# Eight steps of a spiking recurrence take their last rows from SyncE's single-row copies, and the first tables are loaded ahead of those copies

## The chip, the cores and the metric

The kernel runs on one core of one Trainium2 chip. The metric is the time of one execution on the device in microseconds (us), the median over several runs. A profile is one execution taken by the hardware profiler; its span is the time from the first to the last instruction.

In this document PE is TensorE (matrix products and transposes), DVE is VectorE, ACT is ScalarE, POOL is GpSimd and SP is SyncE. SP computes nothing here: it issues DMA transfers, loads registers and waits.

## The reference

`seq` has 1024 rows of 50 item numbers, `emb_table` has 100001 rows of 128 float32 values, `lengths` has 1024 numbers.

```python
emb = emb_table.at[0].set(0.0)
e = emb[seq]                                   # 1024 x 50 x 128: a gather
prefix = jnp.cumsum(e, axis=1)
uF = prefix / minimum(1..T, lengths)           # T = 50
y = batch_norm(uF, over the batch) * gamma + beta
def step(v, x):                                # 50 steps, one after another
    v = v + (x - v) / 2.0
    spike = (v >= 1.0)
    return v - spike * 1.0, spike
uF_out = spikes.mean(axis=0)                   # 1024 x 128
scores = uF_out @ emb.T                        # 1024 x 100001: 409.6 MB
```

## The kernel before, in words

The work has two stages. In the first, 50 steps run in order. In the second, the counts of spikes are multiplied with the whole table, and 409.6 MB of scores are stored.

**A step of the recurrence.** The 1024 sequences stand as eight blocks of 128. `gather(t)` fetches the table rows of step t: for each block GpSimd issues one indirect DMA (line 250) into a tile `e`, 128 rows of 512 bytes. There are two tiles `e` in turn, so the gathers of step t + 2 wait until TensorE has read those of step t. At line 395 TensorE transposes the eight blocks and adds them to the running sums in `pre` (two halves of 512 columns); at line 351 it adds a correction for table row 0. VectorE scales the sums (`uF`, line 409) and takes statistics (412, 424), ScalarE takes the root and the normalized input (428, 435, 458), VectorE updates the potential `v` (367, 370, 461).

**The rows of SyncE.** In the steps listed in `BY_SYNC`, GpSimd gathers seven blocks only. The 128 rows of the eighth block are fetched by SyncE, one DMA for each row (`fetch_singles`, lines 263 to 274). For each 32 rows (`AT_ONCE`) a register load (line 268) brings 32 byte offsets; then each row has a register move and a DMA of 512 bytes (line 271). The rows land in one of four slots of the tile `held_rows`, set i in slot i % 4, and in the step's line 395 TensorE transposes that slot in place of the eighth block. The first set is written into SyncE's queue before step 0; set i + 1 is written into it after step `BY_SYNC[i]`. That is the order within the queue; a later set does not wait for that step on the chip unless its slot is still to be read.

**The table parts.** The table is cut into 98 parts of 1024 rows. The first 40 are loaded by SyncE (line 150), in six groups of six parts, 3072 KB each, and four more parts, and are held on chip until used. `EARLY` tells how many of the six groups are written into SyncE's queue ahead of the first set of single rows. The others follow the last set. At step 44 a further load is written into the queue (line 488) over parts that have been used by then.

**The second stage.** For each part `prepare` transposes it and splits it in two (lines 179, 195, 196). For each part and each of the eight blocks of sequences TensorE makes products (line 203), VectorE and ScalarE scale them in turn into a tile `o` (lines 626, 628), and SyncE stores the tile (line 212). A tile `o` is free again when its store has landed. Later parts are loaded from ScalarE's queue, in places GpSimd picks rows (line 125, with small copies at line 117 between them).

Queues: SyncE's queue takes its DMAs in the order in which the program writes them. The program is scheduled by hand; no planner reorders it.

Of the kernel before, what the change touches and what calls it, by code (L numbers as in the profile page):

```python
# [34 lines left out]
SPLITS = (0, 2, 0, 1, 0, 1, 0, 0)  # L35
PIECES = {(3, 7): 1, (4, 0): 1, (7, 7): 1, (8, 0): 3, (8, 1): 3, (8, 2): 3}

BY_SYNC = (12, 22, 31, 40, 48)
AT_ONCE = 32
EARLY = 2  # L40

SPARED = 120
PICKED = range(42, 97, 3)
# [7 lines left out]
def rec_kernel(  # L51
# [55 lines left out]
    def group(g):  # L107
        at = g if g < AHEAD else AHEAD - 2 + g % 2
        r = rowp.tile([P, GROUP, HALF], F32, tag=f"rows{at}", name=f"rows_{g}")
        for k in range(GROUP):  # L110
            rows[g * GROUP + SHIFT + k if g else k + ASIDE * (k >= TWICE)] = r[:, k, :]
        return r
# [30 lines left out]
    def fetch(r, k, q, n):  # L143

        engine = nc.sync if q < held else nc.scalar
        n = min(n, parts - q)
        whole = n - (size(q + n - 1) < HALF)
        wide = whole - (whole == n and q + whole - 1 in PICKED)
        if wide:
            engine.dma_start(  # L150
                out=r[:, k : k + wide, :],
                in_=table[q * HALF : (q + wide) * HALF, :].rearrange("(q p k) d -> p q (k d)", p=P, k=KQ),
            )
        if wide < whole:
            pick(r[:, k + wide, :], q + wide, engine)
        if whole < n:
            full, rest = divmod(size(parts - 1), KQ)
            c1 = (parts - 1) * HALF
            r = r[:, k + whole, :]
            if rest:  # L160
                at = full - full % 32
                nc.vector.memset(r[at : at + 32, :], 0.0)
                engine.dma_start(
                    out=r[full : full + 1, : rest * D],
                    in_=table[c1 + full * KQ : N, :].rearrange("(o k) d -> o (k d)", o=1),
                )
            if full:
                engine.dma_start(
                    out=r[:full, :],
                    in_=table[c1 : c1 + full * KQ, :].rearrange("(p k) d -> p (k d)", k=KQ),  # L170
                )
# [43 lines left out]
    with ExitStack() as ph:  # L215
# [23 lines left out]
        fetch(first, TWICE, SHIFT, GROUP - TWICE)  # L239
        for g in range(1, EARLY):  # L240
            fetch(group(g), 0, g * GROUP + SHIFT, GROUP)
# [5 lines left out]
        def gather(t):  # L247
            es[t] = gp.tile([P, B], F32, tag="e", name=f"e_{t}")
            for n in range(NB - (t in BY_SYNC)):
                nc.gpsimd.indirect_dma_start(  # L250
                    out=es[t][:, n * P : (n + 1) * P],
                    out_offset=None,
                    in_=table,
                    in_offset=bass.IndirectOffsetOnAxis(ap=idx[:, n, t : t + 1].bitcast(U32), axis=0),
                )
# [7 lines left out]
        def fetch_singles(i):  # L263
            t = BY_SYNC[i]
            rows_of = held_rows[:, i % (BANK // P) * P :][:, :P]
            singles[t] = rows_of
            for p0 in range(0, P, AT_ONCE):
                nc.sync.load(regs, starts[t : t + 1, p0 : p0 + AT_ONCE])  # L268
                for k, reg in enumerate(regs):
                    at = nc.sync.snap(reg, donate=True, min_val=0, max_val=(N - 1) * row_bytes)  # L270
                    nc.sync.dma_start(  # L271
                        out=rows_of[p0 + k : p0 + k + 1, :].bitcast(U8),
                        in_=byte_rows[bass.ds(at, row_bytes)].rearrange("(o b) -> o b", o=1),
                    )
# [112 lines left out]
        for t in range(T):  # L387
# [26 lines left out]
            if t + 2 < T:  # L414
                gather(t + 2)
            if t in BY_SYNC[:-1]:
                fetch_singles(BY_SYNC.index(t) + 1)
                if t == BY_SYNC[-2]:
                    for g in range(EARLY, AHEAD):
                        fetch(group(g), 0, g * GROUP + SHIFT, GROUP)  # L420
# [252 lines left out]
```

## Time and profile before

| | |
|---|---|
| runs | 1722.19, 1728.29 and 1725.5 us, median 1725.5 us |
| the profiled execution | 1711.72 us, span 1710.0 us |
| mean granted clock of TensorE | 0.777 |
| busy: PE, PEld, DVE, ACT, POOL | 1078.7, 816.4, 947.2, 675.8, 432.7 us |
| DMA | 488.23 MB, 286 GB/s on the mean |

How to read it. The page cuts the span into 40 equal slices; a digit is the busy share of an engine in that slice, in tenths. A group line gives the source line, the engine, the operation, output<-input, the count, then busy time and mean ns of one; behind it the idle time before these instructions, and what ended it. A line of the waits gives who waited for whom: total us, times (and the longest). A line of the time order gives start and duration in us, and in square brackets the idle time ahead of it with what ended it; consecutive instructions of one line are merged into one row with a count, which for a queue such as SPq tells from when to when it issued. The instructions of one source line are listed with their shortest, median and longest duration in ns, and the first and last start. A table of windows gives for each stretch its length, each engine's busy time (with the number of instructions), the granted clock, the DMA engines' busy share and the GB/s.

### The profile page before, as it was taken

How to read it: one execution, taken by the hardware profiler on the slowest of the kernel's cores; microseconds unless marked ns; L12 is line 12 of the kernel's file. 1: busy time of each engine (PE TensorE's matmuls, PEld its weight loads, DVE VectorE, ACT ScalarE, POOL GpSimd, SP SyncE). 2: the span in 40 equal slices, each digit the busy share in tenths (PEclk: the TensorE clock that was granted, in tenths of full speed). 3: DMA queues.
4: the chain of work that ended last, by engine and by line, in shares of the span. 5: the costliest groups of instructions: out<-in, count | busy, mean ns of one | idle time of the engine just before them, and what ended most of it. 6: DMA issues, size and time to landing. Idle time of an engine off the chain costs nothing.

```text
span 1710.0 us, 13726 instructions
## 1 busy us (share of the span) xinstructions
PE 1078.7 (63%) x4465; PEld 816.4 (48%) x4465; DVE 947.2 (55%) x1129; ACT 675.8 (40%) x701; POOL 432.7 (25%) x462
## 2 busy tenths in 40 slices
PE   3332331331312416898998888788888888888984
PEld 2111210211211215676777676676666666666763
DVE  4565752773744824556755555555555555555653
ACT  2232321331322413454554444444454444444442
POOL 7666664664664610000000100100100100100000
PEclk7555555555555557999999999898998998999998
DMA  6111111111111129999999999999999999999998
GB/s 223 44 48 47 45 46 34 42 47 32 49 45 34 49 108 409 413 402 423 422 404 430 424 424 426 429 428 423 428 427 426 422 429 424 427 425 430 424 429 379
DMA packets 55612, 488.23 MB, mean 286 GB/s; under 512 B 12527, under 2 KB 13424, under 8 KB 34420
## 3 DMA queue, kind: packets, MB, share of 16 engines
q1 hardware_dynamic: 33472, 431.19, 59.9%
q0 software_dynamic: 16656, 35.60, 7.1%
q10 hardware_dynamic: 5412, 20.56, 2.9%
q8 instruction: 35, 0.57, 0.1%
q14 instruction: 37, 0.30, 0.1%
HBM read 77.69 MB, written 409.60 MB: 285 GB/s over the span
## 4 chain that ended last, share of the span: by engine, by line
DMA 34%; PE 18%; DVE 4%; ACT 3%; issue 3%; SPq 3%; ACTq 0%; DVEq 0%
DMA scores<-o 34%; PE po L203 17%; SPq L271 3%; DVE o L626 3%; ACT o L628 2%; PE pt L179 1%; DVE pairs L196 1%; DMA scores<-two_rows 1%; ACT pairs L195 0%; ACT hi L195 0%; DVE lo L196 0%; SPq L268 0%; PE warm L380 0%; ACT third L195 0%; DVE uF L409 0%
## 5 line engine op out<-in xcount | busy, mean ns | idle before, releaser
L626 DVE TENSOR_SCALAR o<-po 128x1024 f32<-128x1024 f32 x378 | 452.6, 1214 | 322.7 <-DMA scores<-o 158.2
L628 ACT ACTIVATE o<-po 128x1024 f32<-128x1024 f32 x379 | 380.6, 1025 | 494.0 <-DMA scores<-o 324.3
L250 POOL DMA_INDIRECT e<-in_L_rec_emb_table,idx x395 | 375.9, 952 | 228.4 <-issue 110.4
L203 PE MATMUL po<-pairs,countB 128*128 128x512 f32 (+1 forms) x1120 | 290.6, 406 | 42.0 <-ACT o L628 40.3
L203 PE MATMUL po<-pairs,countC 128*128 128x512 f32 (+1 forms) x840 | 242.9, 437 | 60.9 <-ACT o L628 53.7
L203 PEld LDWEIGHTS po<-pairs,countB 128*128 128x128 f32 x1120 | 209.1, 191 | 104.5 <-ACT o L628 55.0
L351 PE MATMUL pre<-zT,ls 128*128 128x512 f32 x100 | 78.6, 788 | 276.7 <-DVE uF L409 176.9
L203 PEld LDWEIGHTS po<-pairs,countC 128*128 128x128 f32 x840 | 169.3, 209 | 114.6 <-ACT o L628 65.1
L409 DVE SCALAR_TENSOR_TENSOR uF<-rlen,pre 128x512 f32<-128x512 f32 (+1 forms) x101 | 68.1, 674 | 235.7 <-PE pre L395 119.2
L125 POOL DMA_INDIRECT rows<-in_L_rec_emb_table,picks x19 | 18.6, 981 | 691.6 <-PE pt L179 688.8
L351 PEld LDWEIGHTS pre<-zT,ls 128*128 128x128 f32 x100 | 29.1, 293 | 317.8 <-DVE uF L409 202.0
L428 ACT ACTIVATE r<-mv,eps 128x1 f32<-128x1 f32 x50 | 14.7, 295 | 346.2 <-DVE mv L424 183.6
L196 DVE TENSOR_TENSOR pairs<-pt,pairs 128x1024 fp32r<-128x1024 f32 x70 | 85.2, 1218 | 96.0 <-ACT pairs L195 95.9
L395 PE MATMUL pre<-ident,e 128*128 128x128 f32 x395 | 102.7, 423 | 25.3 <-DMA e<-in_L_rec_emb_table,idx 13.5
L179 PE MATMUL pt<-ident,rows 128*128 128x128 f32 (+1 forms) x768 | 105.4, 283 | 8.8 <-issue 4.9
L179 PEld LDWEIGHTS pt<-ident,rows 128*128 128x128 f32 (+1 forms) x768 | 95.1, 148 | 25.3 <-issue 11.0
L395 PEld LDWEIGHTS pre<-ident,e 128*128 128x128 f32 x395 | 82.0, 218 | 44.8 <-DMA e<-in_L_rec_emb_table,idx 21.1
L395 PE MATMUL pre<-ident,held_rows 128*128 128x128 f32 x5 | 2.4, 476 | 140.2 <-DMA held_rows<-in_L_rec_emb_table 140.2
L203 PE MATMUL po<-hi,countB 128*128 128x512 f32 x208 | 85.8, 413 | 7.8 <-ACT o L628 7.7
L203 PE MATMUL po<-hi,countC 128*128 128x512 f32 x156 | 69.2, 444 | 27.9 <-ACT o L628 27.0
L195 ACT CAST pairs<-pt 128x1024 fp32r<-128x1024 f32 x70 | 70.0, 1012 | 41.8 <-PE pt L179 41.0
L203 PE MATMUL po<-lo,countB 128*128 128x512 f32 x208 | 83.9, 403 | 0.0
(103 smaller groups left out, 1080.7 us busy)
## 6 DMA issues: line engine op xcount, KB each, us to landing
scores<-o SPq DMA_DIRECT2D x93, 3072.0 KB
scores<-o SPq DMA_DIRECT2D x29, 1536.0 KB
scores<-o SPq DMA_DIRECT2D x28, 1024.0 KB
scores<-o SPq DMA_DIRECT2D x8, 2896.5 KB
rows<-in_L_rec_emb_table ACTq DMA_DIRECT2D x19, 1024.0 KB
rows<-in_L_rec_emb_table SPq DMA_DIRECT2D x5, 3072.0 KB
held_rows<-in_L_rec_emb_table SPq DMA_DIRECT2D x640, 0.5 KB
e<-in_L_rec_emb_table,idx POOLq DMA_INDIRECT x395
```

Source lines behind the costliest of these rows:

```text
L125: nc.gpsimd.indirect_dma_start(out=r, out_offset=None, in_=runs, in_offset=bass.IndirectOffsetOnAxis(ap=which[: r.shape[0], j : j + 1].bit ...
L179: nc.tensor.transpose(pt[:, k0 : k0 + pw], r[:pw, k0 : k0 + D], ident[:pw, :pw])
L195: nc.scalar.copy(vh, vp)
L196: nc.vector.tensor_tensor(vl, vp, vh.bitcast(F32), ALU.subtract)
L203: nc.tensor.matmul(po[:, :kw], lhsT=counts[n], rhs=part[:, k0 : k0 + kw], start=j == 0, stop=j == 1,)
L250: nc.gpsimd.indirect_dma_start(out=es[t][:, n * P : (n + 1) * P], out_offset=None, in_=table, in_offset=bass.IndirectOffsetOnAxis(ap=idx[: ...
L271: nc.sync.dma_start(out=rows_of[p0 + k : p0 + k + 1, :].bitcast(U8), in_=byte_rows[bass.ds(at, row_bytes)].rearrange("(o b) -> o b", o=1),)
L351: nc.tensor.matmul(pre[h], lhsT=l, rhs=zT[:, h * BANK : (h + 1) * BANK], start=t == 0, stop=False, skip_group_check=True,)
L395: nc.tensor.matmul(pre[h][:, k : k + P], lhsT=singles[t] if h * BANK + k + P == B and t in singles else e[:, h * BANK + k : h * BANK + k + P],
L409: nc.vector.scalar_tensor_tensor(uF[:, some], rlen[:, some], 1.0 / (t + 1), pre[h][:, ready], ALU.max, ALU.mult)
L626: nc.vector.tensor_scalar_mul(o[:, h0 : h0 + hw], po[:, :hw], 1.0 / T)
L628: nc.scalar.mul(o[:, h0 : h0 + hw], po[:, :hw], 1.0 / T)
```

## The change

Three more steps take their eighth block from SyncE: eight sets instead of five, used in steps 11 to 48. All six groups of held table parts are written into SyncE's queue ahead of the first set.

```diff
-BY_SYNC = (12, 22, 31, 40, 48)
+BY_SYNC = (11, 17, 22, 28, 33, 38, 43, 48)
 AT_ONCE = 32
-EARLY = 2
+EARLY = 6
```

Where the two are used:

```python
for g in range(1, EARLY):                               # ahead of fetch_singles(0)
    fetch(group(g), 0, g * GROUP + SHIFT, GROUP)
...
for n in range(NB - (t in BY_SYNC)):                    # gather(t): 8 blocks or 7
...
if t in BY_SYNC[:-1]:
    fetch_singles(BY_SYNC.index(t) + 1)
    if t == BY_SYNC[-2]:
        for g in range(EARLY, AHEAD):
            fetch(group(g), 0, g * GROUP + SHIFT, GROUP)
```

With the change SyncE fetches 8 x 128 = 1024 single rows, GpSimd issues 392 gathers instead of 395, and the last loop is empty.

## The prediction

> **What bounds the kernel now.** I read three things in order: the 40 slices of the page, to cut the span into stages; then the waits; then the time order of the waiting queue.
>
> ```profile
> PE   3332331331312416898998888788888888888984
> POOL 7666664664664610000000100100100100100000
> DMA  6111111111111129999999999999999999999998
> ```
>
> Each slice is 42.75 us. For fifteen slices (about 640 us) no engine is full and the DMA engines are nearly idle; that is the recurrence over 50 steps. From slice 16 on the DMA digit is 9; that is the stage that multiplies and stores. What sets the first stage is read from the waits.
>
> ```profile
> PE pre L395 <- DMA held_rows<-in_L_rec_emb_table: 140.2, 5, 34.0
> ...
> 168.31 0.48 PE L395 MATMUL pre<-ident,held_rows 128*128 128x128 f32 x1 [14.87 <-DMA held_rows<-in_L_rec_emb_table]
> 298.89 0.48 PE L395 MATMUL pre<-ident,held_rows 128*128 128x128 f32 x1 [34.04 <-DMA held_rows<-in_L_rec_emb_table]
> 414.79 0.48 PE L395 MATMUL pre<-ident,held_rows 128*128 128x128 f32 x1 [32.49 <-DMA held_rows<-in_L_rec_emb_table]
> 526.70 0.47 PE L395 MATMUL pre<-ident,held_rows 128*128 128x128 f32 x1 [26.31 <-DMA held_rows<-in_L_rec_emb_table]
> 630.29 0.48 PE L395 MATMUL pre<-ident,held_rows 128*128 128x128 f32 x1 [32.50 <-DMA held_rows<-in_L_rec_emb_table]
> ...
> 4.08 1.34 SPq L150 DMA_DIRECT2D rows<-in_L_rec_emb_table  x2
> 7.72 621.57 SPq L271 DMA_DIRECT2D held_rows<-in_L_rec_emb_table  x640
> 629.35 11.94 SPq L150 DMA_DIRECT2D rows<-in_L_rec_emb_table  x4
> ```
>
> At every one of the five steps that use SyncE's rows, TensorE stands still until the rows land: 140.2 us together. The last three rows are SyncE's queue in order of time, and they tell why. It issues 640 single rows without a break from 7.72 to 629.3 us, and the last step that needs them follows at 630.29. So SyncE's rows, and not GpSimd's gathers, set the end of the recurrence. One row costs 621.6/640 = 0.97 us on average, but that average mixes two prices.
>
> ```profile
> L271 SPq DMA_DIRECT2D held_rows<-in_L_rec_emb_table x12: 2/354/1387, 214.2 to 234.1; - x12
> 214.00:236.00 22.00, 5.12 (x16) 3.19 (x16) 16.60 (x18) 0.50 0.20 54
> ...
> L271 SPq DMA_DIRECT2D held_rows<-in_L_rec_emb_table x31: 227/228/229, 288.0 to 297.7; - x31
> 281.00 0.94 POOL L250 DMA_INDIRECT e<-in_L_rec_emb_table,idx  x1 [0.30 <-issue]
> 302.92 0.94 POOL L250 DMA_INDIRECT e<-in_L_rec_emb_table,idx  x1 [20.98 <-PE pre L395]
> ...
> L268 SPq TENSOR_LOAD <-ids x20: 694/1383/2229, 5.5 to 616.7; - x20
> L250 POOL DMA_INDIRECT e<-in_L_rec_emb_table,idx x395 | 375.9, 952 | 228.4 <-issue 110.4
> ```
>
> The first pair is 214 to 236 us, where GpSimd gathers without a gap (18 gathers; the columns before them are TensorE's products and loads): 12 rows go out, 1.83 us each. The next three rows are 288 to 297.8 us, inside a pause of GpSimd from 281.9 to 302.9: 31 rows go out, 9.7/30 = 0.32 us each. So a row is cheap when GpSimd is quiet and about five times dearer beside its gathers. GpSimd is quiet for long only because TensorE waits for rows: both gather buffers are then full.
>
> From this I make two prices. A quiet row is 0.32 us plus its share of the register load that stands ahead of each 32 rows (1.38/32 = 0.04 us); that is 0.37, a floor. I take 0.40, since the queue also stumbles after each load. GpSimd's gathers take 395 x (0.952 + 0.30) = 494 us (0.30 is the issue time in the row at 281.00). Of SyncE's 621 us that leaves 127 quiet us, so 127/0.40 = 318 rows, and the other 322 rows ran beside gathers at 494/322 = 1.53 us. The measured 1.83 of the hardest stretch and 0.40 bracket it.
>
> **The change part by part.**
>
> *Three more held steps.* GpSimd loses three gathers, 3 x 1.25 = 3.8 us, which nothing waits for: it pauses in each of the five waits. SyncE gains 3 x 128 = 384 rows (each a register move and a DMA) and 12 register loads. They go into the queue that sets the end. After: gathers 392 x 1.252 = 491 us, beside which 491/1.53 = 321 rows go out; the other 703 need GpSimd quiet, 703 x 0.40 = 281 us. Together 772 us where 621 us stood: **+151 us**. Put shortly, all additional rows are paid at the quiet price, because the busy time is already used up. Bounds: at the floor of 0.37 on the same rows, 384 x 0.37 = +142; at the mean price of 0.97, +372. I stay by the quiet price, since the gathers do not grow.
>
> *The spacing.* The held steps now lie five or six apart, not nine or ten. Five steps hold about 50 us of gathers (40 x 1.25), beside which 33 of a set's 128 rows go out; the other 95 take 38 us of waiting. That is about 88 us a set against 104 to 131 now. This is the same sum, seen by sets, not another cost. Behind the waiting transpose at L395 stand TensorE's correction products, then VectorE's scaling at L409, and through the gather buffers GpSimd.
>
> *The four slots of the held rows.* With eight sets, the fifth writes over the first one's slot and must wait for step 11's transposes. These lie more than 300 us back by then: nothing. If SyncE were ahead of the steps this would cost a wait, but it is behind.
>
> *Four table loads go ahead of all rows* (groups 2 to 5). They move past the single rows and past the load at L488 on SyncE's queue, and beside the first gathers on GpSimd's.
>
> ```profile
> rows<-in_L_rec_emb_table SPq DMA_DIRECT2D x5, 3072.0 KB
> ...
> 0.00:25.00 25.00, 2.94 (x12) 2.29 (x12) 16.72 (x17) 0.98 0.87 327
> L271 SPq DMA_DIRECT2D held_rows<-in_L_rec_emb_table x7: 3/228/2982, 7.7 to 18.1; - x7
> 25.00:60.00 35.00, 6.69 (x26) 5.53 (x27) 22.98 (x25) 0.50 0.21 60
> L271 SPq DMA_DIRECT2D held_rows<-in_L_rec_emb_table x29: 3/228/717, 27.2 to 59.8; - x29
> ```
>
> Four loads of 3072 KB are 12.6 MB. Now the loads at the start are over at about 25 us (327 GB/s with the gathers in it), and until then SyncE gets out 7 rows, against 29 in the next 35 us. 12.6 MB more at the 327 GB/s of the first 25 us last about 38 us longer, to some 63 us. In that time SyncE loses about 29 rows; they are made up at the quiet price, 29 x 0.40 = 12 us. Some rows will slip through: **+10 us**, between 0 and 38 (38 if the whole stretch is lost with no making up). The gathers keep their rhythm beside loads (17 in the first 25 us). If they did not, the steps would be later, but the first held step waits 14.87 us as it is, and longer after.
>
> *The same loads leave the end of the recurrence.* Here is what they do now.
>
> ```profile
> 630.00:640.00 10.00, 5.13 (x22) 4.20 (x22) 8.34 (x15) 4.02 (x5) 0.00 (x0) 0.67 0.93 359
> 640.00:650.00 10.00, 9.53 (x38) 7.82 (x39) 7.52 (x21) 6.16 (x12) 0.00 (x0) 0.74 1.03 413
> ...
> 648.82 47.39 SPq L212 DMA_DIRECT2D scores<-o  x21
> 653.11 16.18 DMA scores<-o
> ...
> 1000.00:1200.00 200.00, 169.94 (x723) 132.55 (x721) 107.96 (x91) 89.60 (x90) 17.13 (x18) 0.91 1.01 426
> ```
>
> The loads start at 630 and fill the DMA engines (0.93, then 1.03 of them busy). 12.6 MB at 413 GB/s are 31 us, so to about 661. The first stores are issued from 648.82 on by the same queue, behind them, and the chain of waits shows the price: 16.18 us from 653.11 in which the next block waits for a store. Half of the loads, from 630 to 646, lies beside the last step and its sums, where the engines would otherwise idle: it costs nothing now. The other half, some 15 us, delays stores in a stage that is full to its end (1.01 at 426 GB/s), so leaving it out is worth up to 15 us. TensorE must then fill the engines at once, while its granted clock is still 0.74 in that row; I take **-12 us**, between 0 and -17 (the load at L488 goes early as well).
>
> **The sum.** +151 + 10 - 12 = +149 us. The profiled execution took 1711.7 us with a span of 1710.0, so it would become 1861. The three runs have a median of 1725.5 us, 0.8% above the profiled one, and they are what the forecast stands against: 1725.5 + 149 = 1874 us.
>
> **The rivals.**
>
> *Rows that gathers do not hinder (faster).* If the dear rows have another cause, which the change removes, all 1024 rows cost the quiet 0.40: 410 us, less than GpSimd's 491. SyncE is then never late, the five waits go, and so does the delay of the stores: 1725.5 - 140 - 12 = 1573 us. The point from which this decides: SyncE must be done by about 631 us, so 140 quiet us hold 140/0.40 = 350 rows and the other 674 must go out within the 491 us of gathers, at 0.73 us each or less. For it speaks that a row by itself is quick; against it the 12 rows in 22 us beside gathers, when no load was in flight. The Trainium skill, in "DMA: Bandwidth & Descriptors", section "SWDGE vs HWDGE vs iDMA", says that DMAs from the SP queue get their descriptors from dedicated hardware with no software in the loop, while those of GpSimd are written by its own cores; by that rule SyncE's rows should not feel the gathers and this rival would hold. The trace disagrees, 1.83 against 0.32 us, and the measurement decides.
>
> *A flat row price.* If the quick rows come only in bursts that do not grow with the wait, each further row costs the mean: 384 x 0.97 = +372, with the loads 1725.5 + 372 + 10 - 12 = 2096 us. Against it: the 31 rows from 288 to 297.7 have a largest duration of 229 ns; nothing tires there.
>
> *Quiet rows dearer than 0.40.* With pauses cut into eight, more of each is spent before SyncE is at full speed. At 0.50 us, +192 + 12 - 5 = 1925 us.
>
> *A wash.* The 0.73 us just named, or waits that the shorter spacing hides: 1725 us. No row speaks for it.
>
> **How the numbers follow.** Quiet price 0.37 to 0.45 with the loads' bounds: 0.76, that is 1835 to 1910 us. Dearer quiet rows: 0.11. Flat price: 0.06. Unhindered rows: 0.05. A wash: 0.02. The predicted time is that of the first; the range takes in the second and, below, a quiet price near 0.32 together with cheaper busy rows: 1820 to 1950 us. A measurement of this kernel can tell about 0.3% from no change. So faster 0.05, within 0.3% 0.02, slower 0.93.
>
> **What would show it.** SyncE's queue holds 1024 rows from about 10 to about 790 us, and the last held transpose stands at about 790, not 630.3. TensorE's waits on held rows: eight, in total about 300 us, not 140. GpSimd: 392 gathers at the same 0.95 us, with eight long pauses. The DMA share stays high to about 60 us and few rows go out till then. After the last step the first wait on a store is far below 16.18 us, and the stage of stores is shorter by some 12 us at the same 426 GB/s. The prediction is wrong if rows beside gathers go out at well under 1 us, or if the pauses do not lengthen.

## The result, and the profile after

| | before | after |
|---|---|---|
| median of six runs | 1722.89 us | 1850.04 us |
| ratio | | 1.0728, 95% interval 1.0694 to 1.0762 |
| the profiled execution's span | 1710.0 us | 1849.8 us |

The change makes the kernel 127 us slower. First the slices of the page after; a slice is now 46.25 us, and the quiet first stage fills seventeen of them.

```profile
PE   3331302120212213088898988878878888888884
POOL 6663626262616254200000000010010010000000
DMA  9410101010101011069999999999999999999999
```

GpSimd's digit now falls to between 1 and 3 in every second slice or so. These are pauses, and the waits say for what: first the total, then TensorE's held steps with the idle time ahead of each in brackets, then SyncE's queue in order of time, last GpSimd's gathers.

```profile
PE pre L395 <- DMA held_rows<-in_L_rec_emb_table: 348.6, 8, 49.7
...
178.20 0.45 PE L395 MATMUL pre<-ident,held_rows 128*128 128x128 f32 x1 [36.57 <-DMA held_rows<-in_L_rec_emb_table]
272.35 0.45 PE L395 MATMUL pre<-ident,held_rows 128*128 128x128 f32 x1 [45.15 <-DMA held_rows<-in_L_rec_emb_table]
...
787.21 0.45 PE L395 MATMUL pre<-ident,held_rows 128*128 128x128 f32 x1 [43.45 <-DMA held_rows<-in_L_rec_emb_table]
...
4.08 34.82 SPq L150 DMA_DIRECT2D rows<-in_L_rec_emb_table  x6
41.19 744.59 SPq L271 DMA_DIRECT2D held_rows<-in_L_rec_emb_table  x1024
785.89 0.41 SPq L488 DMA_DIRECT2D rows<-in_L_rec_emb_table  x1
...
L250 POOL DMA_INDIRECT e<-in_L_rec_emb_table,idx x392 | 372.7, 951 | 377.6 <-PE pre L395 219.8
```

TensorE waits for rows eight times, 348.6 us in all (140.2 before). SyncE issues its 1024 rows without a break until 785.8, and the last held step follows at 787.21, where it stood at 630.29. From there to the end are 1849.8 - 787.2 = 1062.6 us; before, 1710.0 - 630.3 = 1079.7. So the first stage is 156.9 us longer and the second 17.1 us shorter: +139.8 us between the two profiled executions. The medians differ by 127, mostly because the profiled execution of before lies 11 us below its median; that of the changed kernel lies 1.6 above.

### The profile page after: what moved, and what is told of

Same layout as the page of the kernel before. It is cut to its first block, busy times and chain, and to the rows that moved or that the text cites. A ratio compares the mean times of both kernels' runs of the same rounds, so it can differ in the third digit from the quotient of the medians.

```text
span 1849.8 us, 14514 instructions
## 1 busy us (share of the span) xinstructions
PE 1072.1 (58%) x4465; PEld 811.8 (44%) x4465; DVE 947.9 (51%) x1129; ACT 675.8 (37%) x701; POOL 429.6 (23%) x459
## 4 chain that ended last, share of the span: by engine, by line
DMA 31%; PE 17%; DVE 4%; ACT 3%; issue 2%; SPq 2%; ACTq 0%; DVEq 0%
DMA scores<-o 31%; PE po L203 16%; DVE o L626 2%; ACT o L628 2%; SPq L271 2%; DVE pairs L196 1%; DMA scores<-two_rows 1%; PE pt L179 1%; ACT pairs L195 0%; DVE lo L196 0%; ACT hi L195 0%; SPq L268 0%; PE warm L380 0%; ACT third L195 0%; DMA held_rows<-in_L_rec_emb_table 0%
## 5 line engine op out<-in xcount | busy, mean ns | idle before, releaser
L395 PE MATMUL pre<-ident,held_rows 128*128 128x128 f32 x8 | 3.6, 447 | 348.6 <-DMA held_rows<-in_L_rec_emb_table 348.6
```

The source lines that it names most:

```text
L395: nc.tensor.matmul(pre[h][:, k : k + P], lhsT=singles[t] if h * BANK + k + P == B and t in singles else e[:, h * BANK + k : h * BANK + k + P],
```

## The experiments

Each ratio below is to the kernel before, run beside it on the same chip. There the kernel before took 1712.6 to 1723.6 us, except for e8, e9 and e12, where it took 1553.6; the part on those three says what that means.

**e1 and e2: the two halves of the change.**

```diff
 e1: BY_SYNC = (11, 17, 22, 28, 33, 38, 43, 48), EARLY = 2
 e2: BY_SYNC = (12, 22, 31, 40, 48),             EARLY = 6
```

> Half of the change: eight sets, but the table loads as before. Theory (a row costs 1.53 us beside gathers and 0.40 us when GpSimd is quiet): rows start at 7.7 and take 772 us, not 621, so 1723 + 151 = 1874 us. Rival (the loads ahead hold the rows back by their full 33.5 us, and the rows explain only the rest of the 127 us, that is 127 + 16 - 33.5 = 109): 1832 us.

> The other half: five sets as before, but all loads ahead of the rows. Theory (the late start is mostly made up in the pauses, and the stores gain 16 us): rows from 41 to 634 us, +5 - 16, so 1712 us. Rival (the late start counts in full): +33 - 16, so 1740 us.

e1: 1856.63 us, ratio 1.0756 (1.0730 to 1.0783). e2: 1717.0 us, ratio 0.9968 (0.9939 to 0.9997). SyncE's queue, e1's two rows first, then e2's.

```profile
7.86 771.97 SPq L271 DMA_DIRECT2D held_rows<-in_L_rec_emb_table  x1024
779.89 11.75 SPq L150 DMA_DIRECT2D rows<-in_L_rec_emb_table  x4
...
41.54 609.94 SPq L271 DMA_DIRECT2D held_rows<-in_L_rec_emb_table  x640
651.59 0.41 SPq L488 DMA_DIRECT2D rows<-in_L_rec_emb_table  x1
```

The sets alone make all of the loss. e1's 1024 rows take 772.0 us, and the sum of the prediction had 772; the time still lies 17 us below the theory's 1874 (and 25 above the rival's 1832), which the account below takes up. With the loads ahead as well (the changed kernel) they start 33.3 us later than in e1 and end only 6 us later: the late start is made up in the pauses. e2's rows end at 651.5. That is 22 us later than in the profile of before, which was a quick execution, and 12 later than in e7 below, which has the same sets and the loads of before and takes the same time; the theory had 5 and the rival 33. The time, 1717.0 us, is nearer to the theory's 1712 than to the rival's 1740. Taken together e2 gains 0.3%, since its second stage is 17 us shorter; its interval just excludes no change.

**e3, e4 and e11: no rows, and two sets.**

```diff
 e3, e11: BY_SYNC = (), fetch_singles(0) left out, EARLY = 6
 e4:      BY_SYNC = (24, 47),                      EARLY = 6
```

> No single rows at all, GpSimd gathers all 400 blocks, loads ahead. Theory (SyncE's rows set the end of the recurrence): now GpSimd sets it, 400 x 1.25 = 501 us with some 55 us of its other pauses, end of the recurrence about 73 us sooner, stores 16 us sooner: 1634 us. Rival (the rows relieve GpSimd, as they seem meant to): five gathers more, +6 - 16, so 1713 us.

> Two sets, used in steps 24 and 47, loads ahead. Theory: 128 rows beside gathers take 196 us, so the sets are there at 237 and 433 us, before their steps; no wait on them, and three us fewer of gathers than without rows: 1631 us. Rival (any set costs a wait of some 30 us): 1690 us.

> No single rows, loads ahead, as in e3. Where the kernel before takes about 1723 us: 1632 us again. Where it takes about 1554 us: five gathers more than before, 5 x 1.25, so 1560 us.

e3: 1632.15 us, ratio 0.9449 (0.9419 to 0.9479). e4: 1632.32 us, 0.9469 (0.9443 to 0.9495). e11, on another chip: 1624.34 us, 0.9481 (0.9445 to 0.9517). Of the versions that fetch every row which the reference asks for, these are the fastest here on such chips, ahead of both kernels. Listed by source line, e3's gathers, with what their idle time was, and then e4's rows in SyncE's queue.

```profile
L250 POOL DMA_INDIRECT e<-in_L_rec_emb_table,idx x400: 940/944/1733, 3.6 to 565.7; - x134
  remote: 41.9, 10
...
41.48 341.45 SPq L271 DMA_DIRECT2D held_rows<-in_L_rec_emb_table  x256
```

Without rows the gathers run through from 3.6 to 565.7 us, with 42 us of pauses of their own (the profile names only "remote" as their cause), and the first stage ends about 60 us sooner. So SyncE's rows set its end before. In e4 the 256 rows take 1.33 us each without any long pause of GpSimd (I had 1.53), and come in time, with no wait on them; two gathers less are too little to see. Doing more in SyncE's queue could only help while those rows stay hidden, as two sets do here and five do not; three and four were not run.

**e5, e6 and e7: what makes a row dear.**

```diff
 e5: for n in range(NB // 2): gather        # e[:, k : k + P] in place of e[:, h * BANK + k : ...]
 e6: at = (t * P + p0 + k) * row_bytes      # no register load, no move
 e7: out=es[t][:, n * P : n * P + P // 2]   # from step 2 on, of a table seen as rows of 256 bytes
```

> The kernel before with half of GpSimd's gathers left out (four blocks a step; the other four reuse them), same five sets of rows. Theory (gathers make rows dear): 250 us of gathers hide 163 rows, the other 477 cost 191 us, so rows end at 449 instead of 629 us: 1543 us. Rival (a row costs 0.97 us whatever GpSimd does): 1723 us.

> The kernel before with the rows of SyncE at fixed addresses: no register loads and no register moves, 640 DMAs as before (the values of those blocks are other rows). If beside gathers each instruction of SyncE costs 0.70 us (move and DMA make 1.4): a row costs 0.72 beside gathers, all 640 are hidden, GpSimd sets the end: about 1650 us. If the DMA itself costs 1.53: rows end 32 us sooner by the saved quiet work: 1691 us.

> The kernel before, with GpSimd's gathers of 256 bytes a row instead of 512 from step 2 on (same number of gathers and of rows; the rest of a block is left as it was). If the bytes that the gathers move make SyncE's rows dear: the price falls toward 1 us, about 1648 us. If it is GpSimd's issuing of descriptors: no change, 1723 us.

e5 leaves out half of the gathers: 1451.48 us, ratio 0.8435 (0.8411 to 0.8460). e6 fetches other rows in those blocks: 1625.22 us, 0.9445 (0.9417 to 0.9472). e7 fetches half of each row: 1723.08 us, 1.0007 (0.9979 to 1.0035). SyncE's queue in e5, e6 and e7.

```profile
7.59 299.90 SPq L271 DMA_DIRECT2D held_rows<-in_L_rec_emb_table  x640
...
5.41 485.39 SPq L271 DMA_DIRECT2D held_rows<-in_L_rec_emb_table  x640
...
7.63 631.89 SPq L271 DMA_DIRECT2D held_rows<-in_L_rec_emb_table  x640
```

e7: half the bytes, same price. So what the gathers move is not the cause; their number or their issuing is left. e6: without moves and register loads a row costs 0.76 us, all sets are in time, and GpSimd sets the end. That speaks for a price per instruction of SyncE, though e6 leaves out moves and register loads together and does not tell them apart. Its time is 25 us below the 1650 that I had written; 17 of them are the second stage, since the table loads were issued by 504.8 us, ahead of the last step.

e5 missed my number by 92 us, and shows what is wrong with two fixed prices: 250 us of gathers should have left 640 rows 441 us, and they took 299.9. I then counted in the traces how many row DMAs start between one gather and the next (from 70 us to the last row, mean over runs), by the gather's place in an unbroken run:

| place in the run | 1 | 2 | 3 | 4 | 8 | 11 | 17 |
|---|---|---|---|---|---|---|---|
| before | 3.05 | 2.85 | 2.15 | 1.70 | 0.71 | 0.79 | 0.56 |
| after | 3.37 | 3.11 | 2.00 | 1.84 | 0.60 | 0.93 | 0.50 |
| e5 (runs of four) | 2.97 | 2.94 | 3.03 | | | | |

The first gathers after a pause hardly hurt; beside the later ones a row costs about 2 us. So the price follows the gather's place in its run, and a mean over the runs of 7 to 32 gathers that both kernels have hides that. The pattern stands in these traces; no run on such a chip lengthens or shortens the runs and leaves the number of gathers as it is, as e5 does not. If it holds, a pause pays beyond its own length.

SyncE is not alone in this. The waits of before list VectorE as well:

```profile
DVE uF L409 <- remote: 111.9, 19, 9.1
POOL e L250 <- remote: 54.7, 17, 4.7
```

Ahead of the scaling VectorE's idle time is ended 19 times, after up to 9.1 us, by something that the profile again names only "remote". In e5, with its short runs, no such wait is left on either engine.

**e8, e9, e12: chips on which no row is dear.**

```diff
 e8:      at = RuntimeValue.of_register_unchecked(reg, min_val=0, ...), EARLY = 6
 e9, e12: if n == NB // 2 - 1: 8 x nc.gpsimd.memset(ids[:, 2 * P :], 0.0)
```

> Five sets in the old steps, loads ahead, and the DMA of a row reads its register directly: the register move is left out, the register loads stay. Theory (beside gathers SyncE pays for each instruction, not for the transfer): a row costs about 0.76 us as with fixed addresses, five sets are there in time or nearly, GpSimd sets the end: 1627 us, or up to 1650 if the last set is late. Rival (the register loads, not the moves, were what the fixed addresses saved): as with five sets and loads ahead, 1717 us.

> The kernel before with a pause of GpSimd in the middle of each step (eight small memsets of an unused piece after the fourth gather, some 2 us). Theory (a row's price grows with the length of an unbroken run of gathers: three rows beside the first gather, half a row beside the eighth and later): runs of four let 2.3 rows out beside each gather, SyncE is done with 640 rows by about 340 us, TensorE no longer waits for rows, and GpSimd with its pauses sets the end: between 1690 and 1745 us. Rival (only the total time of the gathers counts, 1.53 us a row, and the pauses add quiet time): SyncE is done at about 625 us and the time is 1723 us.

> The kernel of e9 again (five sets, a pause of 2 us in the middle of each step), since on the chip of e9 no row was held up and there was nothing to relieve. Where the kernel before takes about 1715 us, theory (the price grows with the length of an unbroken run of gathers): SyncE is done with its 640 rows by about 340 us, the rows are not waited for, GpSimd with its pauses sets the end: 1690 to 1745 us. Rival (only the total time of the gathers counts): SyncE is done at about 625 us and the time is that of the kernel before. Where the kernel before takes about 1554 us: 1652 us as in e9.

On two chips the kernel before took 1553.60 and 1553.61 us. e8: 1553.2 us, ratio 0.9997 (0.9987 to 1.0006). e9: 1651.85 us, 1.0637 (1.0619 to 1.0654). e12: 1651.7 us, 1.0628 (1.0611 to 1.0646). e8's edit did not do what it was meant to: its trace still has 640 register moves. It has the five sets and the loads of e2, and as many instructions (13722), so the pair shows the same work on two chips. The moves of SyncE with shortest, median and longest duration in ns, in e2 and then in e8, and e8's queue and gathers.

```profile
L271 SPq MOVE held_rows<-in_L_rec_emb_table x640: 2/29/1407, 41.5 to 651.2; - x160
...
L272 SPq MOVE held_rows<-in_L_rec_emb_table x640: 29/29/29, 41.5 to 317.4; - x160
41.53 276.19 SPq L272 DMA_DIRECT2D held_rows<-in_L_rec_emb_table  x640
L251 POOL DMA_INDIRECT e<-in_L_rec_emb_table,idx x395: 940/944/1727, 3.5 to 497.2; - x198
```

A register move, before which the profile shows no wait, takes up to 1407 ns on the one chip and always 29 on the other. There a row costs 276.19/640 = 0.43 us beside gathers running at the same 944 ns (2.9 rows for each gather of 1.25 us, as beside the first gathers of a run above), the five sets are done at 317.7, and the "remote" waits of GpSimd and VectorE are missing as well: TensorE's longest wait for the scaling is 0.8 us in e8 and 12.3 in e2. So the rows are not all of the difference between the chips: e3, which has none, still takes 79 us longer than e8. With nothing to relieve, the pauses of e9 and e12 only cost their 98 us. So e8, e9 and e12 tell neither of their theories from its rival.

**e10: the change once more.**

> The changed kernel once more, with new runs of the kernel before beside it on the same chip. In the last two kernels SyncE's rows were not held up and the kernel before took 1553.6 us. Theory (how far gathers hold up SyncE's rows differs from chip to chip, and the change loses only where they do): where the kernel before takes about 1723 us, this one takes 1850 us, 7.3% longer; where it takes about 1554 us, TensorE does not wait for rows, three gathers less save 3.8 us, and this one takes 1550 us. Rival (the change loses by the number of rows on any chip): 1554 + 127, so 1681 us.

1829.41 us beside 1712.59, ratio 1.0695 (1.0646 to 1.0743), on the chip of e11. The loss repeats on this chip, where rows are dear too (1024 of them take 719.0 us). The changed kernel was not run on a chip where they are cheap, so its rival there is untested; from e8's 0.43 us a set of 128 would take 55 us in place of the 50 to 60 us of five or six steps, so I estimate that the sets would be nearly hidden and the time near that of before.

## Why the prediction was right

**Which queue ends last.** Right: e3 takes the rows away and the first stage shrinks, e1 adds rows and it grows.

**Rows at the quiet price, +151.** Right in mechanism: there are no more gathers, so each further row is paid in a pause. I counted the rows of the traces by where they start, up to the last row; a long pause is 13 us or more between two gathers, a short one is 1 to 6 us.

| rows, and the time of these stretches | before | e1 | after |
|---|---|---|---|
| in long pauses | 167, 76.5 us | 554, 243.5 us | 573, 249.9 us |
| in short pauses | 51, 59.0 us | 41, 46.5 us | 46, 46.5 us |
| beside gathers | 422, 486.1 us | 429, 481.9 us | 405, 448.2 us |

Outside the long pauses 473 rows go out before and 470 in e1: all 384 additional rows are in long pauses. The sets of the changed kernel follow each other by (787.2 - 178.2)/7 = 87.0 us; the prediction had 88. TensorE's waits came to 348.6 us, where I had written about 300.

The split in the sum was wrong. I had 318 rows in 127 quiet us and 322 beside gathers at 1.53 us. The trace has 167 in 76.5 us of long pauses. Most of the other quiet time is short pauses, in which a row is as dear (1.16 us) as beside gathers (1.15). And a row in a long pause costs 0.44 us, since the first 6 us of each are slow (0.68 us a row in e1) and only then the 0.40 holds.

Of e1's +150.4 us (621.6 to 772.0), +167.0 are long pauses, -12.5 short ones and -4.2 gathers; the prediction had +154 and -3.8. That it came out within 1 us is luck twice: two errors cancel, and the profiled execution of before was quick (11 us under its median) and that of e1 slow (6 us over). Between the medians e1 costs 133 us (1856.63 against 1723.62).

A pause of the changed kernel, by SyncE's row DMAs and by the gathers in a stretch around it:

```profile
L271 SPq DMA_DIRECT2D held_rows<-in_L_rec_emb_table x39: 227/228/268, 605.0 to 620.0; - x39
631.44 0.94 POOL L250 DMA_INDIRECT e<-in_L_rec_emb_table,idx  x1 [35.60 <-PE pre L395]
```

GpSimd stands still for 35.6 us up to 631.44, and 39 rows go out in 15 us of it, 0.39 us each with the register load among them; I had taken 0.40. That the dear price is a mean over long runs did not show here, since the runs of gathers hardly changed; e5 shows it.

**Loads ahead, +10.** About right. Against e1 the changed kernel has 19 rows fewer outside the long pauses and 19 more in them, and its rows end 6 us later; in e2 against e7 it is 25 rows and 12 us. I had 29 rows and 12 us, less what slips out beside the loads. None did:

```profile
25.00:60.00 35.00, 12.71 (x31) 6.39 (x31) 20.13 (x36) 9.84 (x13) 23.11 (x25) 1.00 1.03 391
```

The loads fill the DMA engines to about 60 us as expected (391 GB/s from 25 to 60 us), but issuing them keeps SyncE until 38.9, and the first row goes out at 41.19.

**Stores, -12.** It was -17.1, the bound that I had given. I had doubted that TensorE would fill the DMA engines soon enough at a granted clock of 0.74; from 800 to 820 us it was 0.94 and 1.00, and from 810 on the engines were full (1.02 of them busy). In the chain of waits the first wait on a store is now

```profile
828.99 8.18 DMA scores<-o
```

where it was 16.18 us at 653.11, behind the table loads.

**The rivals.** The flat price (2096 us) and the dearer quiet rows (1925 us) fell with the 772 us of e1. The rows that gathers do not hinder, which I gave 0.05, are what two of the chips show; on the chip of the forecast they were hindered. The dearer quiet rows had a point, the slow start of each pause, but 0.44 us and not 0.50. The Trainium skill, in "DMA: Bandwidth & Descriptors", section "SWDGE vs HWDGE vs iDMA", has SyncE's descriptors made by dedicated hardware with no software in the loop. Read so, a row should feel no gathers, and e8, e9 and e12 agree: 29 ns for every move, a median of 228 ns for a row's DMA. The traces on the other chips disagree wherever rows stand beside long runs of gathers.

**The sum.** +151 + 10 - 12 = +149 against +139.8 between the profiled executions and +127 between the medians. Between medians the parts are +133 for the rows (e1), -17 for the stores (from the last held step to the end 1062.6 us in e2 and in the changed kernel, 1079.6 in e1 and 1079.7 before), and so about +10 for the loads (e2 as a whole is -6.6). Of the 22 us that are missing, about 18 are the rows' term and 5 the stores'. e1's interval alone reaches some 5 us to each side.

## What to carry to other kernels

Before work is moved from one queue to another, find which of the two ends last, and price the move by the queue that takes it: the relief of GpSimd was 3.8 us by my estimate, for which nothing waited, and the load on SyncE cost 133. A mean price per transfer can hide two prices; take it from stretches with and without the neighbour, and ask at which of them the additional work will be paid. And run a tuned kernel on more than one chip: here the same instructions took 1717 us on one and 1553 on another. Five sets were late on the one and in time on the other; what number of sets is best where rows are cheap was not tried.

## What was not expected of the hardware

Beside unbroken gathers, SyncE's instructions, a plain register move among them, were held up by about 0.7 us or a multiple of it (moves of up to 1407 ns in e2); rows fell from three to half of one per gather within about ten gathers and recovered after a pause. VectorE and GpSimd had waits of several us there of which the profile says only "remote". Half the bytes changed nothing (ratio 1.0007), and with half as many gathers in short runs rows cost 0.47 us. On two other chips none of this was seen. What differs between the chips stays open, and so does whether deliberate pauses would help where rows are dear, since e9 and e12 ran where they are not.
